# A causal block convolution with one shared product per head, block halves in a new order, and re-paced shared-expert steps

## The chip, the cores and the metric

The kernel runs on one core of one Trainium2 chip. The metric is the device time of one execution in microseconds (us). Engines are named as in the profile: PE is TensorE (PEld its weight loads), DVE is VectorE, ACT is ScalarE, POOL is GpSimd, SP is the engine that issues most DMAs.

## What is computed

The input x is (8, 256, 512): batch, channels, sequence. All arithmetic is float32. A layer norm gives v. The channels form 32 heads (groups) of 8. In each group every pair (i, j) of channels is multiplied along the sequence, convolved causally with the group's filter k (by FFT in the reference), a skip term is added, and the result is weighed with the context and summed over i:

```python
kv = vr[:, :, :, None, :] * x2r[:, :, None, :, :]
y = causal_conv(kv, k[group]) + kv * skip
out = jnp.einsum('bhijl,bhil->bhjl', y, x1r)      # x1 = x2 = ctx
x = x + out
```

Then comes a mixture of experts on the layer norm of x, for 2048 tokens of width 512: a shared expert of inner width 704, and eight experts of inner width 352, two of them picked for each token with weights from sigmoid scores:

```python
shared = silu(xf @ wg.T) * (xf @ wu.T) @ wd.T
routed = sum over the two picked experts e of weight_e * (silu(xf @ wg_e.T) * (xf @ wu_e.T)) @ wd_e.T
x = x + shared + routed
```

## The kernel before

**Stages.** The conv stage is a Python loop over heads h = 0 to 31 (L835 to L904), with tile t = h // 2 holding two heads. A tail (L907 to L992) finishes the shared expert and the routing, and then 36 to 39 blocks of routed tokens pass through the experts (L1091 to L1123). This text is about the conv stage. The order on each engine is the order in which the program issues instructions[...].

**The convolution as products.** The 512 positions are 4 blocks of 128. Convolution with a filter is multiplication with a lower triangular Toeplitz matrix: out_lb is the sum over mb <= lb of T(lb - mb) times x_mb, where x_mb is kv of block mb (128 positions by 512 columns of batch, j, i). Six of the ten block products lie below the diagonal and are full (128 x 128 matrices, L406). The four on the diagonal are triangular: each is done as a product of all 128 rows with 64 columns and one of 64 rows with 64 columns (diagonal(), L388 to L394), so that pieces for different column halves and row halves of the array can be in it together. Half blocks are stored turned (reversed) or straight, so that one table of half-lag matrices per head, tz (L52 to L56), serves all products: SIN and SOUT say which blocks of the input and output are turned, BIN in which order the input blocks are stored.

**One head.** make_kv (L349) builds kv on GpSimd two heads ahead, four products of 128x512. conv_products (L364) issues 14 products on TensorE into two PSUM tiles of two banks each, pss[0] and pss[1]; their order is at L400. weigh (L409) on VectorE multiplies such a tile with the context (L416, 1024 elements a partition) and sums over i (L425); pss[0] is weighed when its blocks 0 and 1 are done, pss[1] at the end. Between the two weighs VectorE does other work of the head: in odd heads the residual and its statistics (L859 to L867), in even heads the skip's addition and two transposes (L869 to L873), and in some the routing (L874 to L878). At the end of an odd head VectorE sums the skip (skip_sum, L447) and ScalarE turns the halves of that sum (skip_turn, L456, copies at L462).

**The PSUM tiles** of the tag "acc" are three buffers of two banks (L109), given out in order to the conv's two tiles, to each up step and to each pair of down steps. A new owner waits until the earlier owner's readers are done.

**Shared-expert steps.** The tokens come in 4 chunks of 4 tiles. Each chunk has 6 up steps (up_step, L616: 8 products of 128x512 into one PSUM pair; the sixth has half of them), and 4 down steps (down_step, L663: 5 products each, and after each second one two more). An up step's sigmoid is issued on ScalarE at L640; the multiplications that read its PSUM (L643 to L654) are put on the list "owed", and are issued on VectorE by settle() (L705) ahead of the next head's products or of the next step. Chunk c may start in head 8c + 10. The list of steps is L700 to L703, 40 in all, and the loop at L892 issues them so that (h - 9) * 5 // 4 are done after head h: one in most heads, two in every fourth.

**Routing.** For each chunk c, with r = (h - 10) % 8: r = 0 logits, r = 1 a transpose, r = 2 scores and picks (route_scores, route_pick), r = 3 ranks, r = 4 places, with eight scatter DMAs on GpSimd.

The helper that orders the halves on the host, _orders, is at L1126.

Of the kernel before, what the change touches and what calls it, by code (L numbers as in the profile page):

```python
# [8 lines left out]
F32 = mybir.dt.float32  # L9
I32 = mybir.dt.int32  # L10
AF = mybir.ActivationFunctionType
ALU = mybir.AluOpType
# [3 lines left out]
P = 128  # L16
B, D, L = 8, 256, 512
NH = 8
# [26 lines left out]


HP = P // 2
SIN, SOUT = (0, 1, 0, 1), (0, 1, 1, 0)
BIN = (2, 3, 0, 1)


STRAIGHT, TURNED = (6, 7, 2, 3, 2, 5, 4), (4, 5, 3, 2)  # L52
TZ = [(d, d - 1) for d in STRAIGHT] + [(d - 1, d) for d in TURNED] + [(1, 0), (0, 1)]
NTZ = len(TZ) * HP
TZ_AT = {(0, 3): 0, (2, 3): 2, (0, 1): 3, (0, 2): 5, (1, 3): 7, (1, 2): 9}
TZ_10, TZ_01 = 11, 12  # L56
EPS = 1e-5
CTXBUFS, TZBUFS = 5, 3
WARM = 6
# [4 lines left out]
def tile_xattn_moe(  # L64
# [275 lines left out]
        transposed(xfT_of(t), xn2.pop(t).rearrange("p k q a -> p (k q a)"), f"f_{t}")  # L340


    kvs = {}

    def head_cols(h):
        t, hh = divmod(h, 2)
# [2 lines left out]
    def make_kv(h):  # L349
        if h >= H:  # L350
            return
        t, cols = head_cols(h)
        kv = cvp.tile([P, NLB, B, NH, NH], F32, tag="kv", name=f"kv_{h}")
        for mb in range(NLB):
            at = BIN.index(mb)
            G.tensor_tensor(  # L356
                kv[:, mb],
                vT[t][:, at, :, cols].unsqueeze(2).to_broadcast([P, B, NH, NH]),
                ctxT[t][:, at, :, cols].unsqueeze(3).to_broadcast([P, B, NH, NH]),
                ALU.mult,  # L360
            )
        kvs[h] = kv

    def conv_products(h):  # L364
        kv, tz = kvs.pop(h).rearrange("p k b j i -> p k (b j i)"), tzs.pop(h)
        pss = [
            ps_acc.tile([P, 2, B, NH, NH], F32, tag="acc", name=f"cv_{h}_{n}") for n in range(2)
        ]
        banks = [pss[lb // 2][:, lb % 2].rearrange("p b j i -> p (b j i)") for lb in range(NLB)]
        half = slice(0, HP), slice(HP, P)  # L370
        whole = slice(0, P)

        left = [[lb + 1] * 2 for lb in range(NLB)]

        def product(lb, mb, at, rows, cols):
            here = [n for n in range(2) if cols.start <= n * HP < cols.stop]
            first = left[lb][here[0]] == lb + 1
            for n in here:
                left[lb][n] -= 1
            T.matmul(  # L380
                banks[lb][cols],
                lhsT=tz[rows, at * HP : (at + len(here)) * HP],
                rhs=kv[rows, mb],
                start=first,
                stop=left[lb][here[0]] == 0,
            )

        def diagonal():  # L388

            for lb in range(NLB):  # L390
                product(lb, lb, TZ_01 if SIN[lb] else TZ_10, whole, half[1 - SOUT[lb]])

            for lb in range(NLB):
                product(lb, lb, TZ_10 if SIN[lb] else TZ_01, half[SIN[lb]], half[SOUT[lb]])  # L394

        if h == 0:

            order = [(0, 1), (0, 2), (0, 3), (1, 2), (1, 3), None, (2, 3)]
        else:
            order = [None, (0, 1), (0, 2), (1, 2), (0, 3), (1, 3), (2, 3)]  # L400
        for pair in order:
            if pair is None:
                diagonal()
            else:
                mb, lb = pair
                product(lb, mb, TZ_AT[pair], whole, whole)  # L406
        return pss

    def weigh(h, n, ps):  # L409

        t, cols = head_cols(h)
        if h % 2 == 0 and n == 0:
            convT[t] = cvp.tile([P, NLB, B, R], F32, tag="conv", name=f"convT_{t}")
        prod = cvp.tile([P, 2 * B, NH, NH], F32, tag="prod", name=f"prod_{h}_{n}", bufs=1)
        two = slice(2 * n, 2 * n + 2)
        V.tensor_tensor(  # L416
            prod,
            ps.rearrange("p k b j i -> p (k b) j i"),
            ctxT[t][:, 2 + 2 * n : 4 + 2 * n, :, cols]
            .rearrange("p k b i -> p (k b) i")  # L420
            .unsqueeze(2)
            .to_broadcast([P, 2 * B, NH, NH]),
            ALU.mult,
        )
        V.tensor_reduce(  # L425
            convT[t][:, two, :, cols].rearrange("p k b j -> p (k b) j"), prod, AX.X, ALU.add
        )
# [157 lines left out]
    def route_places(c):  # L585
        def rt(name, s=shape, dtype=F32):
            return small.tile(s, dtype, tag=name, name=f"{name}_{c}")

        sel, entry, _ = picks.pop(c)
        ps = ranks.pop(c)  # L590
        pos = ps[:, :TPC]
        V.tensor_tensor(pos, pos, place.unsqueeze(1).to_broadcast(shape), ALU.add)
        V.tensor_tensor(place, place, ps[:, TPC], ALU.add)
        for n in range(2):
            at, to = rt("at"), rt(f"to{n}", [P, TPC], I32)
            V.tensor_tensor(at, pos, sel[n], ALU.mult)  # L596
            with nc.allow_low_precision(reason="whole numbers below 2**14"):
                V.tensor_reduce(to, at, AX.X, ALU.add)
            for i in range(TPC):
                ins = G.indirect_dma_start(  # L600
                    out=table,
                    out_offset=bass.IndirectOffsetOnAxis(ap=to[:, i : i + 1], axis=0),
                    in_=entry[:, i, n, :],
                    in_offset=None,
                    bounds_check=P * NCOL - 1,
                    oob_is_err=True,
                )
                tc.declare_no_dep(ins.ins, group="table", reason="no two rows have one place")
                tc.add_to_no_dep_group("table", ins.ins)
                scatters.append(ins)  # L610
# [52 lines left out]
    def down_step(c, i):  # L663
# [33 lines left out]

        owed.append(rest)

    steps = []  # L700
    for c in range(NCHUNK):
        steps += [(8 * c + 10, up_step, c, ft) for ft in range(NSF)]
        steps += [(8 * c + 10, down_step, c, i) for i in range(TPC)]  # L703

    def settle():  # L705
        while owed:
# [128 lines left out]
    for h in range(H):  # L835
        t, odd = divmod(h, 2)

        load_toeplitz(h + 2)
        if not odd:
            load_tile(t + 3)  # L840
            load_residual(t - 1)
        elif t == NT - 1:
            load_residual(t)
        if h == 3:
            load_shared()

        if not odd:
            first_sums(t + 2)
        elif t + 2 < NT:
            first_norm(t + 2)  # L850
            quarters(("v", t + 2), xv_d[t + 2])
        c, r = divmod(h - 10, 8)
        if c >= 0 and r == 2:
            route_scores(c)
        settle()
        pss = conv_products(h)
        weigh(h, 0, pss[0])
        if odd and t > 0:
            add_residual(t - 1)  # L859
            mv = small.tile([P, V.BN_AGGR_DIM], F32, tag="mv", name=f"mv_{h}")  # L860
            stats(mv, f"2_{t}", x2[t - 1])
            rt = root(f"2_{t}", mv[:, 1:2], 1.0)
            V.reciprocal(rt, rt)
            nb = small.tile([P, 1], F32, tag="nb", name=f"nb2_{t}", bufs=3)
            V.tensor_scalar(nb, mv[:, 0:1], rt, -1.0, ALU.mult, ALU.mult)
            second_norm(t - 1, (rt, nb))
            quarters(("f", t - 1), xn_d[(t - 1) * P : t * P, :])  # L867
        if not odd and t > 0:
            add_skip(t - 1)  # L869
            if t + 1 < NT:  # L870
                square_vT(t + 1)
            if t > 1:
                square_xfT(t - 2)  # L873
        if c >= 0:  # L874
            if r == 2:
                route_pick(c)
            if r == 4:
                route_places(c)  # L878
        weigh(h, 1, pss[1])
        if odd or h == 0:  # L880
            skip_sum(t + odd)
            skip_turn(t + odd)
        if h == 0:
            make_vT(1)

        if not odd:
            skip_spread(t)
        make_kv(h + 2)
        if not odd:
            skip_products(t + 1)  # L890

        while done < min((h - 9) * 5 // 4, len(steps)) and steps[done][0] <= h:  # L892
            settle()
            step()

        if not odd and t > 0:
            residual_T(t - 1)
        if c >= 0:
            if r == 0:
                route_logits(c)  # L900
            if r == 1:
                route_T(c)
            if r == 3:
                route_ranks(c)  # L904
# [221 lines left out]
def _orders():  # L1126

    import numpy as np

    l = np.arange(L).reshape(NLB, 2, HP)  # L1130
    ins = [l[mb, ::-1] if SIN[mb] else l[mb] for mb in BIN]
    outs = [l[lb, ::-1] if SOUT[lb] else l[lb] for lb in range(NLB)]
    return [np.concatenate(o).reshape(L) for o in (ins, outs)]


# [76 lines left out]
```

## Time and profile before

| | us |
|---|---|
| median of 3 runs | 814.59 (814.1 to 818.03) |
| profiled execution, device time | 815.22 |
| its span, first to last instruction | 813.5 |
| TensorE busy in the span | 787.3 |
| VectorE busy | 504.3 |
| GpSimd busy | 431.0 |
| ScalarE busy | 167.0 |
| conv products (L380), busy | 267.9, in 896 records |
| up steps (L626) / down steps (L670), busy | 156.4 / 70.6 |
| first conv product to last conv product starts | 9.9 to 444.4 |

A line of the timeline gives start, duration, engine, source line, operation, output tile <- input tiles, shape of the first instruction, and x the number of records that it merges. A float32 product is two records on TensorE. A line of the waits reads: engine, tile and line that waited <- engine, tile and line that ended the wait: total us, how often, longest. In groups of instructions, the number after the bar is busy time, then the mean of one in ns.

### The profile page before, as it was taken

The page shows a single profiled execution, that of the slowest core. Times are in us where ns is not written, and L with a number is a line of the kernel's source. Part 1 is how long each engine was busy: PE and PEld are TensorE (multiplying, and loading weights), DVE is VectorE, ACT ScalarE, POOL GpSimd, SP SyncE. Part 2 cuts the span into 40 slices and gives each one's busy share as a digit, 9 for nine tenths or more (in the row PEclk, how much of TensorE's full clock was granted, in tenths as well). Part 3 has the DMA queues.
Part 4 walks back from the last instruction along what each step waited for, and adds up shares of the span by engine and source line. Part 5 has one row for each costly group of instructions (what it writes and reads, how often), then busy time and mean ns, then how long its engine had stood idle before and what let it go on. Part 6 is the DMA issues. An engine that isn't in the chain of part 4 may idle for free. (4 is left out here: it accounts for less than half of the span.)

```text
span 813.5 us, 8376 instructions
## 1 busy us (share of the span) xinstructions
PE 787.3 (97%) x2423; PEld 364.9 (45%) x2423; DVE 504.3 (62%) x1165; ACT 167.0 (21%) x317; POOL 431.0 (53%) x430
## 2 busy tenths in 40 slices
PE   7999999999999999999999999999999999999991
PEld 4333334443434443434344344455555555555550
DVE  2869856655545736744647243359888788788850
ACT  2222233332204132113111110001111111111110
POOL 7767752319550508723504012766777777777521
PEclk9999999999999999999999999999999999999996
DMA  6486433214433122431110392267444334443332
GB/s 231 153 295 205 159 127 114 80 60 70 148 113 119 52 87 60 152 106 58 49 52 4 142 427 95 71 209 199 75 75 74 66 75 75 75 74 69 65 42 31
DMA packets 52141, 90.14 MB, mean 111 GB/s; under 512 B 8832, under 2 KB 24064, under 8 KB 50944
## 3 DMA queue, kind: packets, MB, share of 16 engines
q1 hardware_dynamic: 36960, 62.82, 23.0%
q0 software_dynamic: 10816, 18.92, 12.7%
q10 hardware_dynamic: 4320, 7.87, 3.2%
q8 instruction: 21, 0.34, 0.2%
q14 instruction: 24, 0.20, 0.1%
HBM read 67.39 MB, written 22.18 MB: 110 GB/s over the span
## 5 line engine op out<-in xcount | busy, mean ns | idle before, releaser
L380 PE MATMUL cv<-kv,tz 128*128 128x512 f32 (+2 forms) x896 | 267.9, 608 | 1.8 <-POOL kv L356 1.8
L955 POOL DMA_INDIRECT xg<-xn_d,src x144 | 147.2, 1022 | 57.9 <-issue 39.4
L1014 PE MATMUL up<-wgu_sb,xT 128*128 (+1 forms) x576 | 176.1, 459 | 0.0
L356 POOL TENSOR_TENSOR kv<-vT,ctxT 128x512 f32<-128x512 f32 x128 | 132.5, 1068 | 72.5 <-issue 67.5
L380 PEld LDWEIGHTS cv<-kv,tz 128*128 128x128 f32 (+2 forms) x896 | 93.1, 158 | 162.9 <-issue 151.7
L626 PE MATMUL gu<-xfT,wsh 128*128 128x512 f32 x352 | 156.4, 599 | 0.3
L1058 DVE STREAM_TRANSPOSE hTb<-h 32x96 f32<-32x96 f32 (+1 forms) x560 | 146.3, 261 | 8.2
L1014 PEld LDWEIGHTS up<-wgu_sb,xT 128*128 128x128 f32 x576 | 109.2, 190 | 70.5 <-issue 16.4
L416 DVE TENSOR_TENSOR prod<-cv,ctxT 128x1024 f32<-128x1024 f32 x64 | 77.9, 1217 | 69.3 <-PE cv L380 69.2
L626 PEld LDWEIGHTS gu<-xfT,wsh 128*128 128x128 f32 x352 | 66.9, 192 | 85.6 <-issue 82.6
L600 POOL DMA_INDIRECT table<-entries,to x32 | 31.9, 998 | 135.4 <-DVE at L596 126.9
L1072 PE MATMUL y<-wd_sb,hTb 128*128 (+3 forms) x216 | 98.6, 593 | 0.8 <-ACT hTb L1047 0.8
L1081 POOL DMA_INDIRECT out_dram<-ys,row x36 | 58.2, 1617 | 44.2 <-ACT ys L1080 20.5
L425 DVE TENSOR_REDUCE convT<-prod 128x128 f32<-128x1024 f32 x64 | 78.1, 1220 | 2.2
L670 PE MATMUL dn<-wshd,hT 128*128 128x512 f32 x160 | 70.6, 593 | 0.0
L1072 PEld LDWEIGHTS y<-wd_sb,hTb 128*128 128x128 f32 (+1 forms) x216 | 41.0, 190 | 43.1 <-issue 34.7
L643 DVE TENSOR_TENSOR sg<-sg,gu 128x512 f32<-128x512 f32 (+1 forms) x24 | 16.4, 684 | 64.9 <-ACT sg L640 64.9
L1022 ACT ACTIVATE h<-up 128x352 f32<-128x352 f32 x36 | 16.7, 464 | 164.2 <-PE up L1014 164.2
L640 ACT ACTIVATE sg<-gu 128x512 f32<-128x512 f32 (+1 forms) x24 | 14.3, 596 | 173.4 <-PE gu L626 173.4
L470 POOL TENSOR_TENSOR skip<-ctxT,w 128x512 f32<-128x512 f32 x16 | 18.2, 1136 | 59.0 <-ACT w L462 58.9
L670 PEld LDWEIGHTS dn<-wshd,hT 128*128 128x128 f32 x160 | 30.2, 190 | 37.6 <-issue 37.6
L1023 DVE TENSOR_TENSOR h<-h,up 128x352 f32<-128x352 f32 x36 | 18.6, 517 | 41.3 <-ACT h L1022 41.3
(136 smaller groups left out, 430.7 us busy)
## 6 DMA issues: line engine op xcount, KB each, us to landing
tz<-in_toep_dram SPq DMA_DIRECT2D x32, 416.0 KB, 3.3
wgu_sb<-in_egu_dram SPq DMA_DIRECT2D x8, 1408.0 KB, 17.6
ctxT<-in_cT_dram SPq DMA_DIRECT2D x16, 384.0 KB, 5.0
x<-in_xv_dram SPq DMA_DIRECT2D x16, 256.0 KB, 3.6
x<-in_x_dram SPq DMA_DIRECT2D x16, 256.0 KB, 4.9
xn_d<-xn ACTq DMA_DIRECT2D x16, 256.0 KB, 2.0
out_dram<-x SPq DMA_DIRECT2D x16, 256.0 KB, 2.3
wd_sb<-in_ed_dram SPq DMA_DIRECT2D x8, 512.0 KB, 11.0
```

The costliest lines, as they stand in the source:

```text
L356: G.tensor_tensor(kv[:, mb], vT[t][:, at, :, cols].unsqueeze(2).to_broadcast([P, B, NH, NH]), ctxT[t][:, at, :, cols].unsqueeze(3).to_broa ...
L380: T.matmul(banks[lb][cols], lhsT=tz[rows, at * HP : (at + len(here)) * HP], rhs=kv[rows, mb], start=first, stop=left[lb][here[0]] == 0,)
L416: V.tensor_tensor(prod, ps.rearrange("p k b j i -> p (k b) j i"), ctxT[t][:, 2 + 2 * n : 4 + 2 * n, :, cols] .rearrange("p k b i -> p (k b ...
L425: V.tensor_reduce(convT[t][:, two, :, cols].rearrange("p k b j -> p (k b) j"), prod, AX.X, ALU.add)
L600: ins = G.indirect_dma_start(out=table, out_offset=bass.IndirectOffsetOnAxis(ap=to[:, i : i + 1], axis=0), in_=entry[:, i, n, :], in_offse ...
L626: T.matmul(ps, lhsT=wsh[:, k, m0 : m0 + m], rhs=rhs[k], start=(k == 0), stop=(k == NLB - 1))
L670: T.matmul(ps, lhsT=hTs[c][:, ft, i * P : (i + 1) * P], rhs=wshd[:, ft, :], start=(ft == 0), stop=False,)
L955: G.indirect_dma_start(out=xgs[k][:, c, :], out_offset=None, in_=xn_q, in_offset=bass.IndirectOffsetOnAxis(ap=src[:, c, k : k + 1], axis=0 ...
L1014: T.matmul(ps[:, m, :FF], lhsT=xTs[k][:, j].rearrange("p c b -> p (c b)"), rhs=wk[:, bass.ds(eks[k] * NGU + (m * NLB + j) * FF, FF)], star ...
L1058: V.transpose(hT[q * Q : (q + 1) * Q, :n, c], hk[c * Q : (c + 1) * Q, q * NF * Q : (q * NF + n) * Q].rearrange("p (t a) -> p t a", a=Q),)
L1072: T.matmul(ps, lhsT=hT[:fw, ft].rearrange("p c b -> p (c b)"), rhs=wk[:fw, bass.ds(eks[k] * NWD + ft * L, L)], start=(ft == 0), stop=(ft = ...
L1081: G.indirect_dma_start(out=out, out_offset=bass.IndirectOffsetOnAxis(ap=row[:, k : k + 1], axis=0), in_=y, in_offset=None, bounds_check=NT ...
```

## The change

From head 10 (H9) on, two of the six full products, T2 x0 (for block 2) and T2 x1 (for block 3), become one product, T2 (x0 + x1), in a PSUM tile "same" of its own. What that adds wrongly is put right in the T1 and T3 products: block 2 gets (T1 - T2) x1 in place of T1 x1, block 3 gets (T3 - T2) x0 in place of T3 x0. So five full products are issued rather than six.

- GpSimd makes x0 + x1 (ks) and the two differences (td, with two buffers) at the end of make_kv.
- ScalarE copies "same" to SBUF, once straight for block 2 and once with its halves swapped for block 3, since block 3's output is stored the other way round.
- VectorE adds these copies to the banks of blocks 2 and 3 at the start of weigh.
- The half blocks are laid out anew (SIN, BIN, a new BOUT, the table TZ with 12 entries rather than 13), so that x0 and x1 are stored straight. One PSUM tile now holds blocks 0 and 2, the other blocks 1 and 3.
- In heads 1 to 9 the order is diagonal, (0,2), (1,2), (0,1), (0,3), (1,3), (2,3). From head 10 it is: the shared product, (0,1), (2,3), (T3 - T2) x0, diagonal, (T1 - T2) x1.
- From head 10 VectorE does both weighs after the head's other work, pss[1] first; in heads with route_pick the transpose of xf comes after them.
- The first two chunks' down steps are issued two at a time, which makes 36 steps, and the loop issues one step a head, two in the last.

```diff
-SIN, SOUT = (0, 1, 0, 1), (0, 1, 1, 0)
-BIN = (2, 3, 0, 1)
-STRAIGHT, TURNED = (6, 7, 2, 3, 2, 5, 4), (4, 5, 3, 2)
+SIN, SOUT = (0, 0, 1, 1), (0, 1, 1, 0)
+BIN, BOUT = (1, 3, 0, 2), (0, 2, 1, 3)
+STRAIGHT, TURNED = (6, 7, 4, 5, 3, 2, 5, 4), (2, 3)
...
-TZ_AT = {(0, 3): 0, (2, 3): 2, (0, 1): 3, (0, 2): 5, (1, 3): 7, (1, 2): 9}
-TZ_10, TZ_01 = 11, 12
+TZ_AT = {(0, 3): 0, (1, 3): 2, (0, 1): 4, (1, 2): 4, (0, 2): 6, (2, 3): 8}
+TZ_10, TZ_01 = 10, 11
+H9 = 10
...
         kvs[h] = kv
+        if h >= H9:
+            ks = rows.tile([P, L], F32, tag="xg", name=f"ks_{h}")
+            flat = kv.rearrange("p k b j i -> p k (b j i)")
+            G.tensor_tensor(ks, flat[:, 0], flat[:, 1], ALU.add)
+            td = cvp.tile([P, 2, P], F32, tag="td", name=f"td_{h}", bufs=2)
+            tb = tzs[h][:, : 4 * P].rearrange("p (n m q) -> p n m q", n=2, m=2)
+            G.tensor_tensor(td, tb[:, :, 0], tb[:, :, 1], ALU.subtract)
+            kss[h] = ks, td
...
+        nine = h >= H9
+        if nine:
+            ks, td = kss.pop(h)
+            same = ps_acc.tile([P, 2, L], F32, tag="acc", name=f"same_{h}")[:, 0]
+        pss = {
+            n: ps_acc.tile([P, 2, B, NH, NH], F32, tag="acc", name=f"cv_{h}_{n}")
+            for n in ((1, 0) if nine else (0, 1))
+        }
...
-            order = [None, (0, 1), (0, 2), (1, 2), (0, 3), (1, 3), (2, 3)]
+            order = [(0, 1), (2, 3)]
+            T.matmul(same, lhsT=of(TZ_AT[0, 2]), rhs=ks, start=True, stop=True)
+            again, turned = [
+                rows.tile([P, L], F32, tag="xg", name=f"{name}_{h}") for name in ("same", "turned")
+            ]
+            for n in range(2):
+                A.copy(turned[half[n]], same[half[1 - n]])
+            A.copy(again, same)
+            boths[h] = {2: again, 3: turned}
...
+        if nine:
+            product(3, td[:, 0], kv[:, 0])
+            diagonal()
+            product(2, td[:, 1], kv[:, 1])
         return pss
...
+        for i, lb in enumerate(BOUT[2 * n : 2 * n + 2]):
+            if lb in boths.get(h, ()):
+                bank = ps[:, i].rearrange("p b j i -> p (b j i)")
+                V.tensor_tensor(bank, bank, boths[h].pop(lb), ALU.add)
...
+    def down_steps(c, i, n):
+        for j in range(i, i + n):
+            down_step(c, j)
+
     steps = []
     for c in range(NCHUNK):
         steps += [(8 * c + 10, up_step, c, ft) for ft in range(NSF)]
-        steps += [(8 * c + 10, down_step, c, i) for i in range(TPC)]
+        n = 2 if c < NCHUNK - 2 else 1
+        steps += [(8 * c + 10, down_steps, c, i, n) for i in range(0, TPC, n)]
...
-        weigh(h, 0, pss[0])
+        nine, picks_here = h >= H9, c >= 0 and r == 2
+        if not nine:
+            weigh(h, 0, pss[0])
...
+        if nine:
+            weigh(h, 1, pss[1])
+            weigh(h, 0, pss[0])
+            if picks_here:
+                square_xfT(t - 2)
+        else:
+            weigh(h, 1, pss[1])
...
-        while done < min((h - 9) * 5 // 4, len(steps)) and steps[done][0] <= h:
+        while done < h - 9 + h // (H - 1) and steps[done][0] <= h:
```

More of the change, by code (lines that the diff above doesn't have):

```diff
@@ L340, in make_xfT @@
         transposed(xfT_of(t), xn2.pop(t).rearrange("p k q a -> p (k q a)"), f"f_{t}")
-    kvs = {}
+    kvs, kss, boths = {}, {}, {}
     def head_cols(h):
@@ L362, in make_kv, with product @@
         kvs[h] = kv
+        if h >= H9:
[6 more added lines that the diff above has]
+            kss[h] = ks, td
     def conv_products(h):
         kv, tz = kvs.pop(h).rearrange("p k b j i -> p k (b j i)"), tzs.pop(h)
[L366 to L369, printed above, removed]
+        nine = h >= H9
[6 more added lines that the diff above has]
+        }
+        places = [BOUT.index(lb) for lb in range(NLB)]
+        banks = [pss[n // 2][:, n % 2].rearrange("p b j i -> p (b j i)") for n in places]
         half = slice(0, HP), slice(HP, P)
         whole = slice(0, P)
-        left = [[lb + 1] * 2 for lb in range(NLB)]
-        def product(lb, mb, at, rows, cols):
+        total = [1, 2, 2, 3] if nine else [1, 2, 3, 4]
+        left = [[n] * 2 for n in total]
+        def product(lb, w, x, cols=whole):
             here = [n for n in range(2) if cols.start <= n * HP < cols.stop]
-            first = left[lb][here[0]] == lb + 1
+            first = left[lb][here[0]] == total[lb]
             for n in here:
@@ L381, in product @@
                 banks[lb][cols],
-                lhsT=tz[rows, at * HP : (at + len(here)) * HP],
-                rhs=kv[rows, mb],
+                lhsT=w,
+                rhs=x,
                 start=first,
@@ L386, in product, with of @@
             )
+        def of(at, n=2, rows=whole):
+            return tz[rows, at * HP : (at + n) * HP]
         def diagonal():
             for lb in range(NLB):
-                product(lb, lb, TZ_01 if SIN[lb] else TZ_10, whole, half[1 - SOUT[lb]])
+                product(lb, of(TZ_01 if SIN[lb] else TZ_10, 1), kv[:, lb], half[1 - SOUT[lb]])
             for lb in range(NLB):
-                product(lb, lb, TZ_10 if SIN[lb] else TZ_01, half[SIN[lb]], half[SOUT[lb]])
+                rows = half[SIN[lb]]
+                at = TZ_10 if SIN[lb] else TZ_01
+                product(lb, of(at, 1, rows), kv[rows, lb], half[SOUT[lb]])
         if h == 0:
             order = [(0, 1), (0, 2), (0, 3), (1, 2), (1, 3), None, (2, 3)]
-        else:
-            order = [None, (0, 1), (0, 2), (1, 2), (0, 3), (1, 3), (2, 3)]
+        elif not nine:
+            order = [None, (0, 2), (1, 2), (0, 1), (0, 3), (1, 3), (2, 3)]
+        else:
+            order = [(0, 1), (2, 3)]
[7 more added lines that the diff above has]
+            boths[h] = {2: again, 3: turned}
         for pair in order:
@@ L405, in conv_products @@
                 mb, lb = pair
-                product(lb, mb, TZ_AT[pair], whole, whole)
+                product(lb, of(TZ_AT[pair]), kv[:, mb])
+        if nine:
+            product(3, td[:, 0], kv[:, 0])
+            diagonal()
+            product(2, td[:, 1], kv[:, 1])
         return pss
@@ L411, in weigh @@
         t, cols = head_cols(h)
-        if h % 2 == 0 and n == 0:
+        if t not in convT:
             convT[t] = cvp.tile([P, NLB, B, R], F32, tag="conv", name=f"convT_{t}")
+        for i, lb in enumerate(BOUT[2 * n : 2 * n + 2]):
+            if lb in boths.get(h, ()):
+                bank = ps[:, i].rearrange("p b j i -> p (b j i)")
+                V.tensor_tensor(bank, bank, boths[h].pop(lb), ALU.add)
         prod = cvp.tile([P, 2 * B, NH, NH], F32, tag="prod", name=f"prod_{h}_{n}", bufs=1)
@@ L871, in tile_xattn_moe @@
                 square_vT(t + 1)
-            if t > 1:
+            if t > 1 and not picks_here:
                 square_xfT(t - 2)
[L874 to L879, printed above, removed]
+        if picks_here:
+            route_pick(c)
+        if c >= 0 and r == 4:
+            route_places(c)
+        if nine:
+            weigh(h, 1, pss[1])
+            weigh(h, 0, pss[0])
+            if picks_here:
+                square_xfT(t - 2)
+        else:
+            weigh(h, 1, pss[1])
         if odd or h == 0:
@@ L1131, in _orders @@
     ins = [l[mb, ::-1] if SIN[mb] else l[mb] for mb in BIN]
-    outs = [l[lb, ::-1] if SOUT[lb] else l[lb] for lb in range(NLB)]
+    outs = [l[lb, ::-1] if SOUT[lb] else l[lb] for lb in BOUT]
     return [np.concatenate(o).reshape(L) for o in (ins, outs)]
```

## The prediction, made before the changed kernel ran

> **What bounds the kernel now.** I read the busy shares first, then what TensorE waited for, then its work in order of time around one head.
>
> ```profile
> PE 787.3 (97%) x2423; PEld 364.9 (45%) x2423; DVE 504.3 (62%) x1165; ACT 167.0 (21%) x317; POOL 431.0 (53%) x430
> ```
>
> A busy share alone could mislead, so the next question is whether TensorE ever waits. These are all its waits in the span:
>
> ```profile
> PE slots_ps L788 <- DVE by_quarter L776: 2.0, 1, 2.0
> PE cv L380 <- POOL kv L356: 1.8, 1, 1.8
> PE ptf L272 <- ACT xn_kqa L328: 1.6, 1, 1.6
> PE warm L819 <- POOL filler L143: 1.3, 1, 1.3
> PE ptr L486 <- DVE convT L478: 1.1, 1, 1.1
> PE ptv L272 <- ACT xn L267: 1.0, 1, 1.0
> PE y L1072 <- ACT hTb L1047: 0.8, 1, 0.8
> ```
>
> They come to 9.6 us in 813.5, and none lies in heads 10 to 31 (106 to 445 us). There the end is set by how many products TensorE is given. The timeline of TensorE (start, duration, x records) prices them; this is head 20 and the step after it:
>
> ```profile
> 258.34 8.30 PE L380 MATMUL cv<-kv,tz 128*64 128x512 f32 x28
> 266.48 7.03 PE L626 MATMUL gu<-xfT,wsh 128*128 128x512 f32 x16
> 273.35 0.60 PE L486 MATMUL ptr<-ident,convT 128*128 128x128 f32 x4
> 273.88 8.30 PE L380 MATMUL cv<-kv,tz 128*64 128x512 f32 x28
> ```
>
> Use starts, since ends overlap. An up step is 8 products in 16 records, so a float32 product is two records: (273.35 - 266.48)/8 = **0.859 us** a product. A head's conv is 8.14 us; less six products (5.15) the diagonal costs 2.99, where its four 128x64 and four 64x64 products would need 2.58 if two, or four, ran at once. So they do run together, with 0.4 us of switching.
>
> The last view is the end of an odd head on ScalarE (head 19), which the pace of the steps will touch:
>
> ```profile
> 254.65 0.45 ACT L462 COPY w<-w 64x32 f32<-64x32 f32 x2 [2.16 <-DVE w L452]
> 255.11 1.28 ACT L640 ACT_TABLE_LOAD   x1
> 258.01 0.60 ACT L640 ACTIVATE sg<-gu 128x512 f32<-128x512 f32 x1 [1.61 <-PE gu L626]
> ```
>
> The sigmoid of an odd head's step stands behind skip_turn's copies, which stand behind VectorE's skip_sum, which stands behind the last weigh; then the table load. Here TensorE is still later (1.61 us idle), so nothing is lost.
>
> [...]the eight diagonal products take 2.99 us, not 8 x 0.859. [...] The trace has the 1.28 and no further gap: a square root follows its load at once (170.60 + 1.28, next at 171.89). [...] L490, 128x512 from PSUM, takes 676 ns, and I use that for the new adds.
>
> **The change part by part.**
>
> *Products.* Heads 10 to 31 issue 13 products instead of 14, with the diagonal's eight unchanged in number and shape: 22 x 0.859 = **-18.9 us**, all on TensorE's path. Heads 0 to 9 keep 14. The new order of halves changes the order of the four 64x64 tiles from (0,0),(1,1),(0,1),(1,0) to (0,0),(0,1),(1,1),(1,0): still four different tiles and four banks. I take zero; bounds: zero, and the rival below. A gain is excluded but for the 0.4 us of switching, whose number of switches is the same.
>
> *Added on GpSimd.* x0 + x1 (128x512) like L356, 1.07 us; T1 - T2 and T3 - T2 (128x256) between half of that and all of it, say 0.6: 1.7 us a head. GpSimd needs about 12.2 us in two heads of some 30, and has kv two heads ahead; both hide. The new wait, td for its slot until head h's last product, has only skip_products and the next kv behind it, due a head later.
>
> *Added on ScalarE.* Three copies from PSUM like L507 (0.59, started every 0.5): 1.6 us a head. They free "same", whose buffer the step's product takes at 7.28 us after the conv's start (8.14 - 0.86). In even heads the queue ahead is sigmoid and sums, over at about 4.1; free at 5.8. In a head with route_scores (12, 20, 28) another load and sigmoid precede, and the odd head's late sigmoid (below) shifts the sums: free near 7.6, so TensorE waits 0.3 x 3 = **+0.9**.
>
> *Added on VectorE.* Two adds of 0.68 a head. A weigh is now 0.70 + 1.25 + 1.14 = 3.1 us. Take the conv's start as 0: the diagonal ends at 3.43 + 2.99 = 6.42, weigh 1 runs 6.6 to 9.7, weigh 0 to 12.8 (its bank read out by 11.7). The next head asks for that bank at 0.86 into its conv. With a full step that is 7.28 + 6.87 + 0.86 = 15.0: covered by 3.3 us of the step; without a step it would cost 3.6 a head. With route_pick ahead (4.0 us, from 5.9 on) it is read out by 15.0, asked for at 15.5: still covered.
>
> *The pace.* One step a head puts the short sixth up step (four products, 3.43 us) in heads 15, 23 and 31, **odd** heads. Before it fell to even heads (177.37, 305.02). Now follow the chain in head 15: weigh 0 ends 12.8, skip_sum 0.68 to 13.5, skip_turn 0.45 to 13.95, table load to 15.25, sigmoid to 15.85, VectorE's three products of L643 and L649 (0.69 + 0.86) to **17.5**. Only then is the step's PSUM free. TensorE has ended conv and step at 10.7, and head 16's fifth product group, the diagonal, asks for that buffer at 10.7 + 3.43 = **14.1**. It waits 3.4 us with the whole queue behind it. Heads 15 and 23: **+6.7**; head 31 has no skip_sum and no head after it, so nothing. Other odd heads with up steps (11, 13, 19, 21, 27, 29) have the same chain, ending near 17.3, and the next diagonal due at 18.1 or later: 0.8 us of cover. Bounds of one stall: 0 (if head 16 were served by another buffer) and 5 us (if copies and adds run slower).
>
> *Moved.* The down pairs are the same products in heads 16, 17, 24, 25 rather than spread; their outputs' DMAs on SP's queue stand behind the same Toeplitz load. The table shrinks from 13 to 12 columns of halves (416 to 384 KB a head): DMA is not waited for, 0. In heads 1 to 9 weigh 0 starts one product later (0.86): the one wait there, 1.1 us at L486, ends a VectorE backlog that began at a DMA wait, so 0. After head 31 the same 13 steps are left (40 - 27 before, 36 - 23 after), all shifted; the experts' weights land before a product waits for them (no wait at L1014).
>
> **Sum:** -18.9 + 6.7 + 0.9 = -11.3. The profiled execution took 815.2 (span 813.5 and 1.7 around it): 803.9. The median of the runs is 0.6 lower: **803.3**.
>
> **Rivals.**
>
> *A, as summed*, 803.3, with its own range 800 to 806.5.
>
> *B, the short step's chain is covered*: something in it starts earlier than I queue it. Then only the products count: 814.6 - 18.9 = 795.7. For it: TensorE loses nothing now. Against: the order on ScalarE shown above.
>
> *C, the VectorE and ScalarE chain is about 1 us longer than I count* (adds and copies meeting GpSimd's added work; L478, without PSUM, varies from 0.68 to 1.59 us). Then six more odd heads lose 0.2 each, heads 15 and 23 one more each, the three routing heads one more each: + 6.2, 809.5. Against: VectorE's busy share is 62%.
>
> *D, slower: the four 64x64 tiles lose their overlap.* In the new order neighbours share rows or columns; before, first and second, third and fourth shared neither. If they went two by two, each of 32 heads pays one product more, 32 x 0.86 = 27.5: 831. It decides from 0.35 us a head on, where it eats the 11.3. Against: the 128x64 products share all rows and overlap.
>
> That the change does not do what it says is excluded: 13 products are issued where 14 were.
>
> **How the numbers follow.** A 0.57, B 0.17, C 0.20, D 0.06. Half a percent, about what a measurement can tell here, is 4.1 us: 810.5 to 818.7 is "same". A and B are faster, C in six parts of ten: 0.86. The rest of C, 0.08, is same; D 0.06 is slower. The range takes A whole, most of B and C: 796 to 809.8.
>
> **What would show it.** TensorE's timeline: heads from 10 on at 26 records and 7.3 us; 2.99 for the diagonal unchanged in all heads (else D). TensorE's waits: a wait of 3 to 4 us at the diagonal of heads 16 and 24 for VectorE's L649 (none: B; also at heads 12, 14, 20: C), and small ones at the steps of heads 12, 20, 28 for the copies. VectorE's new adds at 0.68. GpSimd never ahead of a TensorE wait. I am wrong if a wait for td or the sum appears, or if the tail after head 31 is not merely shifted.

## The result and the profile after

| | before | changed |
|---|---|---|
| median, us (4 runs each) | 816.31 (814.1 to 818.29) | 807.03 (806.57 to 809.01) |
| ratio to before, 95% interval | | 0.9892 (0.9855 to 0.9929) |
| profiled execution: device time / span | 815.22 / 813.5 | 809.01 / 807.2 |
| from the first transpose of a residual (tile 0) to the last tile's transpose "ptf", in the trace | 423.6 | 417.3 |

The change makes the kernel 1.1% faster: 9.3 us, where 11.3 were forecast. The last row, the **conv stage** below, covers heads 3 to 31. It leaves out the first heads and the tail, where the granted clock of TensorE (the share of full speed that it is given) differed between the two profiled executions: its mean was 0.84 from 9 to 20 us before and 0.73 from 9 to 21.5 us after, 0.83 in the tail before (503 to 513 us) and 1.00 after (500 to 507 us).

The shares of busy time in the changed kernel:

```profile
PE 774.5 (96%) x2379; PEld 355.0 (44%) x2379; DVE 532.8 (66%) x1209; ACT 212.8 (26%) x389; POOL 473.2 (59%) x474
```

TensorE gave up 44 records, two for each of 22 products. Its busy time fell by 12.8 us, its span by 6.3: the rest is in new waits. These are the first two of all its waits (engine, tile and line that waited <- who ended the wait: total us, times, longest):

```profile
PE cv L398 <- DVE hT L693: 6.2, 2, 3.1
PE gu L670 <- ACT same L435: 2.1, 3, 1.5
```

The first is the wait that the sum had priced at 6.7 us. Of the second, 1.5 us lie in head 10, which the sum had not looked at. TensorE's timeline shows head 11, which follows the logits; head 13 with the transposes ahead of it; then the short step of head 15 and the conv of head 16:

```profile
116.06 1.06 PE L543 MATMUL pl<-xfT,gw_sb 128*32 128x512 f32 x8
117.06 1.12 PE L429 MATMUL same<-ks,tz 128*128 128x512 f32 x2
...
124.54 7.03 PE L670 MATMUL gu<-xfT,wsh 128*128 128x512 f32 x16
...
146.67 0.60 PE L530 MATMUL ptr<-ident,convT 128*128 128x128 f32 x4
147.10 1.02 PE L429 MATMUL same<-ks,tz 128*128 128x512 f32 x2
147.97 1.88 PE L398 MATMUL cv<-kv,tz 128*128 128x512 f32 x4
149.68 1.02 PE L398 MATMUL cv<-kv,td 128*128 128x512 f32 x2
150.63 2.96 PE L398 MATMUL cv<-kv,tz 128*64 128x512 f32 x16
153.52 1.13 PE L398 MATMUL cv<-kv,td 128*128 128x512 f32 x2
154.48 7.03 PE L670 MATMUL gu<-xfT,wsh 128*128 128x512 f32 x16
...
184.52 3.60 PE L670 MATMUL gu<-xfT,wsh 128*128 128x512 f32 x8
187.96 1.02 PE L429 MATMUL same<-ks,tz 128*128 128x512 f32 x2
188.83 1.98 PE L398 MATMUL cv<-kv,tz 128*128 128x512 f32 x4
190.65 1.02 PE L398 MATMUL cv<-kv,td 128*128 128x512 f32 x2
194.76 5.60 PE L398 MATMUL cv<-kv,tz 128*64 128x512 f32 x16 [3.09 <-DVE hT L693]
200.29 1.23 PE L398 MATMUL cv<-kv,td 128*128 128x512 f32 x2
```

Head 13 takes 154.48 - 147.10 = 7.38 us, against 8.14 before: 0.76 less, not 0.86. The transposes ahead of it take 147.10 - 146.67 = 0.43, against 273.88 - 273.35 = 0.53 before: there is the other 0.1. Head 11 takes 124.54 - 117.06 = 7.48. Head 16 stops at its diagonal for 3.1 us, as predicted, and then the sixteen records of the diagonal last 5.53 us in place of 2.89. That second loss was not in the prediction. The view by stretches shows what it is (its columns: busy time of PE, PEld, DVE, ACT and POOL with the number of instructions, then TensorE's granted clock, DMA share, GB/s):

```profile
21.50:190.00 168.50, 166.09 (x556) 63.71 (x555) 126.15 (x184) 61.46 (x124) 115.12 (x109) 1.00 0.45 146
...
194.70:201.00 6.30, 6.24 (x18) 1.63 (x19) 2.36 (x4) 3.33 (x5) 4.96 (x5) 0.54 0.18 66
```

After the wait the granted clock is about half: 0.54 in this stretch, 1.00 in the first. The cause of the wait is read on ScalarE, the end of head 15, and on VectorE:

```profile
190.66 0.45 ACT L506 COPY w<-w 64x32 f32<-64x32 f32 x2 [7.05 <-DVE w L496]
191.12 1.28 ACT L684 ACT_TABLE_LOAD   x1
192.41 0.59 ACT L684 ACTIVATE sg<-gu 64x512 f32<-64x512 f32 x1
```

```profile
189.95 0.68 DVE L496 TENSOR_REDUCE w<-skip 128x64 f32<-128x512 f32 x1
193.04 0.68 DVE L687 TENSOR_TENSOR sg<-sg,gu 64x512 f32<-64x512 f32 x1 [2.42 <-ACT sg L684]
193.75 0.86 DVE L693 TENSOR_TENSOR hT<-sg,gu 64x256 f32<-64x256 f32 x2
```

The step's products were over at about 188.1 (TensorE began the next head at 187.96). Their sigmoid starts at 192.41, behind the copies and the table load, and VectorE frees the PSUM at 194.6; TensorE goes on at 194.76.

**Theories.** Theory 1: the gain is the 22 products; what is missing of it is the odd head's queue behind a short step, because four tiles a head now go round three PSUM buffers and the conv therefore takes the step's buffer. Rival 2: VectorE, with both weighs at the head's end, is simply late, whatever ScalarE does. Others stand with the runs.

### The profile page after: what moved, and what is told of

It reads as the page before. It is cut to its first block, busy times and chain, and to the rows that moved or that the text cites. A ratio compares the mean times of both kernels' runs of the same rounds, so it can differ in the third digit from the quotient of the medians.

```text
span 807.2 us, 8497 instructions
## 1 busy us (share of the span) xinstructions
PE 774.5 (96%) x2379; PEld 355.0 (44%) x2379; DVE 532.8 (66%) x1209; ACT 212.8 (26%) x389; POOL 473.2 (59%) x474
## 3 DMA queue, kind: packets, MB, share of 16 engines
q0 software_dynamic: 10816, 18.92, 12.9%
## 5 line engine op out<-in xcount | busy, mean ns | idle before, releaser
L398 PE MATMUL cv<-kv,tz 128*64 128x512 f32 (+2 forms) x720 | 197.8, 629 | 8.0 <-DVE hT L693 6.2
L1073 PEld LDWEIGHTS up<-wgu_sb,xT 128*128 128x128 f32 x576 | 109.2, 190 | 70.5 <-issue 16.6
L398 PEld LDWEIGHTS cv<-kv,tz 128*64 128x64 f32 (+2 forms) x720 | 62.5, 154 | 131.6 <-issue 111.1
L460 DVE TENSOR_TENSOR prod<-cv,ctxT 128x1024 f32<-128x1024 f32 x64 | 78.1, 1221 | 21.8 <-PE cv L398 20.2
L469 DVE TENSOR_REDUCE convT<-prod 128x128 f32<-128x1024 f32 x64 | 78.1, 1220 | 2.2
L398 PE MATMUL cv<-kv,td 128*128 128x512 f32 x88 | 47.4, 620 | 0.0
L1139 ACT ACTIVATE ys<-y,gate 128x512 f32<-128x512 f32 x36 | 24.8, 688 | 78.3 <-PE y L1131 75.3
```

The lines of the kernel that those rows point to most:

```text
L398: T.matmul(banks[lb][cols], lhsT=w, rhs=x, start=first, stop=left[lb][here[0]] == 0,)
L460: V.tensor_tensor(prod, ps.rearrange("p k b j i -> p (k b) j i"), ctxT[t][:, 2 + 2 * n : 4 + 2 * n, :, cols] .rearrange("p k b i -> p (k b ...
L469: V.tensor_reduce(convT[t][:, two, :, cols].rearrange("p k b j -> p (k b) j"), prod, AX.X, ALU.add)
L1073: T.matmul(ps[:, m, :FF], lhsT=xTs[k][:, j].rearrange("p c b -> p (c b)"), rhs=wk[:, bass.ds(eks[k] * NGU + (m * NLB + j) * FF, FF)], star ...
```

## The experiments

Each kernel was compared with the kernel before on the same chip. There were three chips, on which the kernel before had medians of 814.8, 823.6 and 834.0 us; so across chips only ratios and conv stages compare (e1 to e4 ran on the first, e5 to e8 on the second, e9 to e12 on the third). Each conv stage is read from one trace. "Waits" are TensorE's in the conv stage, us, without those of up to 1 us ahead of the transposes. e1's and e2's edits are called the two mends.

| run | edit | median / before | ratio (95%) | conv stage | waits for L693, L689 | other waits |
|---|---|---|---|---|---|---|
| e1 | short step even, all chunks | 802.72 / 814.78 | 0.9854 (0.9826 to 0.9882) | 407.3 | 0.8 | copies 2.1 |
| e2 | turn after the step | 797.87 / 814.78 | 0.9810 (0.9774 to 0.9845) | 408.5 | 1.2 | copies 1.5 |
| e3 | copies first in even heads | 809.16 / 814.78 | 0.9925 (0.9898 to 0.9953) | 414.4 | 6.4 | 1.2 in head 10 |
| e4 | pace alone, on the kernel before | 816.55 / 814.78 | 1.0011 (0.9996 to 1.0025) | 422.1 | 0 | 0 |
| e5 | both mends | 809.44 / 823.56 | 0.9820 (0.9794 to 0.9846) | 405.8 | 0 | copies 1.5 |
| e6 | first weigh not last | 861.84 / 823.56 | 1.0462 (1.0432 to 1.0493) | 458.5 | 10.2 | 30 |
| e7 | shared product in the other pool | 811.40 / 823.56 | 0.9844 (0.9822 to 0.9867) | 407.3 | 0 | 3.7 |
| e8 | shared product from head 4 | 836.50 / 823.56 | 1.0149 (1.0122 to 1.0175) | 430.4 | 6.2 | 19 |
| e9 | the changed kernel again | 822.27 / 834.03 | 0.9860 (0.9821 to 0.9899) | 414.1 | 6.2 | copies 2.1 |
| e10 | short step even, three chunks | 814.36 / 834.03 | 0.9760 (0.9722 to 0.9799) | 407.6 | 0.8 | copies 2.1 |
| e11 | e2 again | 818.85 / 834.03 | 0.9807 (0.9762 to 0.9851) | 408.3 | 1.2 | copies 1.5 |
| e12 | e5 again | 811.52 / 834.03 | 0.9739 (0.9696 to 0.9782) | 406.2 | 0 | copies 1.5 |

**e1: the short step in an even head.**

```diff
-        steps += [(8 * c + 10, up_step, c, ft) for ft in range(NSF)]
+        steps += [(8 * c + 10, up_step, c, ft) for ft in (0, 1, 2, 3, 5, 4)]
```

> The changed kernel with one edit: each chunk's up steps go in the order 0, 1, 2, 3, 5, 4, so the short step falls on an even head (r = 4) and a full one on the odd head (r = 5). Theory 1 (the stall is the odd head's queue: weighs, skip_sum, skip_turn, table load, sigmoid, then the products that free the step's PSUM): no wait of TensorE for VectorE's L693 (6.2 us before the edit), so no half clock after it (about 4.3 us in the profiled execution): 797 to 801 us. Rival 2 (VectorE is simply late after two weighs at the head's end, whatever ScalarE does): a wait of about 3 us at the diagonal moves to the heads after r = 4, time unchanged near 807.

The waits of 3.1 us went; 0.53 and 0.3 us are left, and after the first of these the diagonal takes 191.73 - 188.85 = 2.88 us, so no half clock follows it. The conv stage is 10 us shorter. Rival 2 falls for the even heads: in head 14 VectorE has two weighs at the end too, and freed the short step's PSUM at 173.72, 0.28 us before the next diagonal started. Odd heads, where skip_sum comes on top, are left to e2. The time, 802.72, is above the 797 to 801 expected. A reason lies in the tail: there the same edit puts the short step beside the load of the routing table, and TensorE waits for that load.

```profile
PE slots_ps L836 <- DMA tab<-table: 3.5, 1, 3.5
```

**e2: the turn after the step.**

```diff
-            skip_turn(t + odd)
+            if not nine:
+                skip_turn(t + odd)
...
+        if nine and odd:          # after the loop that issues the step
+            skip_turn(t + 1)
```

> The changed kernel with skip_turn's two copies issued after the head's step instead of before it, from head 10 on; nothing else. Theory 1: the sigmoid of heads 15 and 23 comes 0.2 us after its products (10.9 us after the conv's start, not 15.3), VectorE's products then only wait for skip_sum (13.5) and end near 15.1, one us after the diagonal asks: each of the two waits falls from 3.1 to about 1 us, and with it the half clock after it: 799 to 803 us. Rival 2: waits stay at 3.1, 807.

On ScalarE, the end of head 15 in this run:

```profile
180.97 1.28 ACT L684 ACT_TABLE_LOAD   x1 [0.39 <-ACT xn L269]
185.14 0.59 ACT L684 ACTIVATE sg<-gu 64x512 f32<-64x512 f32 x1 [2.88 <-PE gu L670]
187.64 0.44 ACT L506 COPY w<-w 64x32 f32<-64x32 f32 x2 [1.91 <-DVE w L496]
```

The table is loaded early and the sigmoid waits for nothing but its products. TensorE's wait at the diagonal of head 16 is now 0.58 us, for VectorE's skip_sum and the two weighs ahead of the products. VectorE has the same work in the same order as in the changed kernel, so of 3.1 us, 2.5 were ScalarE's queue, and Rival 2 is left with the 0.58. The waits for the copies in heads 12 and 20 fell from 0.3 to about 0.1, as expected if the odd head's late sigmoid had pushed them.

**e3: the copies ahead of the statistics.**

```diff
         if not odd:
-            first_sums(t + 2)
+            if h < H9:
+                first_sums(t + 2)
...
         pss = conv_products(h)
+        if not odd and h >= H9:
+            first_sums(t + 2)
```

> The changed kernel with the even heads' statistics of the next tile (first_sums, ScalarE) issued after the conv's products, so the copies of the shared product stand ahead of them. Theory 1: TensorE's three waits for the copies (L435, 2.1 us, longest 1.5 in head 10) go, the two waits for L693 stay at 3.1: 805 us. Rival 3 (these waits are ScalarE's total load): they come back at another line of ScalarE, 807.

Neither a gain of 2 us nor a loss can be told from the changed kernel here (the intervals overlap). In heads 12 and 20 the wait is gone. In head 10, where it was 1.48, 1.17 is left: the copies now end at 105.0 and the step starts at 106.87, for its input xf is transposed on VectorE until 106.77. One wait had covered another. In the changed kernel this transpose ends at 108.22, 0.3 us ahead of the step, after a wait for a DMA:

```profile
107.51 0.71 DVE L296 STREAM_TRANSPOSE xfT<-xq_f 128x512 f32<-128x512 f32 x1 [2.13 <-DMA xq_f<-xn_d]
```

(For head 10 of this run the profile names ScalarE's L253, which ended at about the same time. At the two diagonals, 3.2 us stand against the copy L435. VectorE's L693 ended 0.2 us before that copy, at 192.31, so that one or the other releases.)

**e4: the pace alone, in the kernel before.** The edit is the change's down_steps, its list of steps and its "h - 9 + h // (H - 1)", without the shared product.

> The kernel before, with only the new pace: down steps by twos in the first two chunks and one step a head, two in the last. Theory 1: the late products of the odd head matter only because four tiles a head now go round three PSUM buffers, so that the conv's tile takes the step's buffer; here three tiles a head go round three buffers and a step only waits for the step before: no wait of TensorE at the conv, time as before, 816 within 2. Rival 4 (the pace itself costs): waits of about 3 us at heads 16 and 24, 820 or more.

No wait and no difference. The pace costs nothing that can be told by itself; it needs the fourth tile to cost something.

**e7: the shared product in another pool.** This takes the fourth tile out of the three buffers and leaves the pace.

```diff
-            same = ps_acc.tile([P, 2, L], F32, tag="acc", name=f"same_{h}")[:, 0]
+            same = ps_tp.tile([P, L], F32, tag="tp", name=f"same_{h}")
```

> The changed kernel with the shared product's PSUM tile taken from the two one-bank buffers of the transposes instead of the three pairs of banks, so that again three tiles a head go round three buffers there. Theory 1: no wait for L693 and none for the copies at the steps (8.3 us of waits go, and the half clock after them); new waits of about 2.3 us at the shared product in heads 11, 19 and 27, whose buffer the residual of the head before still holds: 801 to 804. Rival 2 (VectorE late by itself): waits at the diagonal of heads 16 and 24 stay, 810 or more.

The waits for L693 are gone, and new ones stand at the shared product of heads 11, 19 and 27, at 0.75 each instead of 2.3. I had named the residual as the reader that holds the buffer. The times name another: the shared product starts at 116.00, 237.71 and 359.41, each 0.1 us after ScalarE's copy of the logits (L551) ends, while the residual of head 11 is read until 116.49. In head 10 a wait of 1.4 us stays although no copy holds the step's buffer: as in e3, xf is late there (its transpose ends at 106.61, the step starts at 106.71). With e4 this settles that the buffer's rotation joins the conv to the step.

```profile
PE same L429 <- issue: 2.3, 3, 0.8
PE gu L670 <- issue: 1.4, 1, 1.4
```

**e6: the first weigh where it was.** The weigh of blocks 1 and 3 is issued right after the products; the rest of the head's work, square_xfT included, follows, then the other weigh.

> The changed kernel with one part undone: from head 10 on the first weigh (blocks 1 and 3) stands where it stood before, ahead of the head's other VectorE work, and only the second stands last. VectorE then sits idle until the diagonal ends (6.6 us into the conv) and does the other work after it. Theory 1, by queue: the first up step of a chunk waits for its input, transposed at about 11.8 and asked for at 7.3 (heads 10, 18, 26: 4.5 each), heads with picks 2 each, odd heads 1.2 to 1.8, heads 15 and 23 5.8: in all some 40 us of waits against 8.3, about 835 to 850. Rival 5 (VectorE has so much time that its order does not matter): 807 to 812.

TensorE's waits in the conv stage come to 40 us, as queued, though 6.8 of them are at a place I had not named, the shared product waiting for GpSimd's sum. A lower clock came on top: its mean from 100 to 470 us was 0.96, and the step after the wait of 5.97 us took 122.14 - 112.41 = 9.73 us against 6.87. The kernel is 4.6% slower than the one before. This order of VectorE's work carries the change.

```profile
PE gu L670 <- DVE xfT L296: 8.5, 2, 4.3
PE same L429 <- POOL ks L368: 6.8, 2, 3.5
PE gu L670 <- issue: 6.0, 1, 6.0
PE cv L398 <- DVE hT L689: 5.9, 5, 1.5
PE cv L398 <- DVE hT L693: 4.3, 2, 2.8
```

**e8: from head 4 on**, H9 = 4 and nothing else.

> The changed kernel with the shared product from head 4 on instead of head 10. Heads 4 to 9 have no step beside them. If only products counted: six heads by 0.7, 803. Theory 1 (the step is the cover of VectorE's work): VectorE needs 15.4 us for two such heads now and 18.2 with the four new adds, TensorE 15.5: VectorE sets the pace, 18.2 against 16.9 without the shared product, so 3 times 1.3 more: 810 to 813, with waits of TensorE for VectorE's weighs in heads 5 to 9.

Expected was a time 2 to 5 us below the kernel before (810 to 813 against 814.8); it is 12.9 us above. Heads 8 and 9 (78.1 to 99.1 us) take 21.1 us, not 18.2. VectorE is busy for only 16.6 of 21: its queue stands still behind ScalarE, 2.0 us for the turned copy in each even head and 2.0 for the root in each odd one, since both stand behind other work there.

```profile
DVE rstd L917 <- ACT rstd L244: 6.5, 4, 2.1
DVE cv L457 <- ACT turned L434: 6.1, 3, 2.0
```

That VectorE's work is uncovered without a step holds (10.2 us of TensorE's waits are for its L460); the size was off by ScalarE's part.

**e5: both mends**, with e1's order in the first three chunks only.

> The changed kernel with both mends: skip_turn's copies after the step (as in the run with the late turn), and the short step in the even head in the first three chunks only, so that the last chunk keeps a full step beside the load of the table. Theory 1: no wait for VectorE over 0.5 us at heads 15 to 16 and 23 to 24, the wait for the table stays at 2 us, one wait of 1.5 us in head 10: 796 to 798 us, about 1 us below the late turn alone. Rival 2 (VectorE late by itself): waits of 1 us or more stay at the diagonal, 798 or more.

No wait for VectorE is left in the conv stage, which is 17.8 us shorter than before. The time is 14.1 us below the kernel before, where 17 to 19 were expected (796 to 798 against the first chip's 814.8): in the trace TensorE waits 4.9 and 3.6 us at the start of the experts' blocks.

**e9 to e12** put the changed kernel and the mends on one chip.

> The changed kernel itself, once more, as the measure for the three runs beside it on one chip: 1.0 to 1.4 per cent below the kernel before, two waits of 3.1 us for L693 and 2.1 us for L435.

> The changed kernel with the short up step in an even head in the first three chunks, the last chunk in its old order; skip_turn stays before the step. Theory 1: as with the short step even in all chunks, waits for L693 gone (0.5 us at most left, for L689), but the wait for the table, 3.5 us there, falls back to about 2 and no half clock follows: 1 to 4 us below that run, 8 to 9 us below the changed kernel. Rival (the table's load was late by chance there): the same time as with all four chunks, 12 us below the kernel before.

> The changed kernel with skip_turn's copies after the step, again, beside the other two mends on one chip: 8 to 9 us below the changed kernel, waits of 0.6 us at heads 16 and 24 and none above 0.2 at heads 12 and 20.

> The changed kernel with both mends, beside each alone on one chip. Theory 1: the late turn has already taken 2 x 2.5 of the 2 x 3.1 us and the short waits of heads 12 and 20, so the second mend adds about 1.2 us: 9 to 10 us below the changed kernel. If the two waits were separate causes, their gains would add: 16 us below.

e9 repeats the changed kernel's gain (1.4%) and its waits. By medians on that chip e10, e11 and e12 lie 7.9, 3.4 and 10.8 us below the changed kernel, where 8 to 9, 8 to 9, and 9 to 10 were expected; by conv stage 6.5, 5.8 and 7.9. In the conv stage the mends do not add (6.5 + 5.8 = 12.3 against 7.9): they are two ways past one queue. The medians alone do not show it (7.9 + 3.4 = 11.3 against 10.8). In e12 head 16 runs through:

```profile
186.34 1.02 PE L429 MATMUL same<-ks,tz 128*128 128x512 f32 x2
187.20 1.88 PE L398 MATMUL cv<-kv,tz 128*128 128x512 f32 x4
188.91 1.02 PE L398 MATMUL cv<-kv,td 128*128 128x512 f32 x2
189.87 2.96 PE L398 MATMUL cv<-kv,tz 128*64 128x512 f32 x16
```

e11 gained less in time than in the conv stage: in its trace TensorE waits 11.6 us at the start of the experts' blocks. Waits there come to 6 to 12 us in every trace of the second and third chip, e12's too, and to 1.4 at most on the first. Their cause stays open: in e5 and e12 an add of L739 on VectorE starts 10 and 19 us late, with no releaser that the program shows. In e10 the wait for the table fell from 3.5 us (e1) to 0.5, but the tail was shorter by 0.9 us only; why was not shown.

e12 has the lowest ratio to the kernel before, 2.6% faster, though its interval overlaps e10's; against the changed kernel on that chip it is 1.3% faster by medians.

## Why the prediction was right

The direction, the mechanism and the place of the largest loss were right; the gain was forecast 2.0 us too large. (The time itself, 807.03, lies 3.7 us above the forecast, 1.7 of them because the median of the kernel before rose from 814.59 to 816.31 with its fourth run. It also lies just above the range of Rival A, 800 to 806.5.) In the two profiled executions the sum was further off: -6.3 against -11.3. Term by term, with each wait counted from the start that was due, 0.1 to 0.2 us longer than its idle time:

- **Products**, -18.9 forecast, -17.4 measured. The step that failed is "whose number of switches is the same". It holds where transposes stand ahead of the head: the switch of tile form into the diagonal moved from them into the head, where the full product before the diagonal lasts 150.63 - 149.68 = 0.95 in place of 0.86 (the one after it, 154.48 - 153.52 = 0.96, took as long in the kernel before), and 0.76 + 0.1 is the 0.86 of the forecast. It fails where a product of another form stands ahead, the logits or the down steps' last products: it was followed by the diagonal and is now followed by a full product, which is one switch more. Five such heads take 7.48 us, 0.2 above the forecast 7.28; the three after the ranks lose 0.1 each.
- **Pace**, +6.7 forecast (its own terms add up to 17.4 rather than 17.5 us, that is 6.5): +6.3 in two waits, at the heads and for the reason given. The half clock after them (granted 0.54 from 194.7 to 201.0 us, 0.76 from 320 to 327), +2.7 and +1.6 us (the stretch from the diagonal to the next step, 6.59 and 5.45 against 3.85), was **left out**. It is the largest error of the sum.
- **Copies**, +0.9 forecast for heads 12, 20 and 28: 0.5, 0.5 and none (no statistics are due in head 28), but 1.6 in head 10, which I had not looked at. There xf is late as well, as e3 and e7 show, so the copies' own part is about 0.3. Together +2.6.
- **Order of the tiles** (D), 0: the diagonal lasts 2.89 us in the changed kernel. D is out. B is out with the waits; C's further waits did not come.
- **GpSimd**, hidden: no wait behind td or ks, though the sum took 1.29 us and not 1.07, and the differences 0.73 and not 0.6.
- **Not counted**: waits of 0.8 us in the kernel before (for xf at heads 10, 18 and 26) and 1.4 us at L486 and L328 shrank or went; and the clock outside the conv stage, which cost 1.8 us more in the first head (0.73 against 0.84) and 1.7 us less in the tail (1.00 against 0.83). I take this last pair for chance, which was not shown.

-17.4 + 6.3 + 4.3 + 2.6 - 0.8 - 1.4 = -6.4, against 417.3 - 423.6 = -6.3 for the conv stage; the first head and the tail cancel, and the spans differ by -6.3 too. The medians give -9.3: the changed kernel's profiled execution was the slowest of its four (809.01, with a granted clock of 0.982 against 0.984 to 0.986 in the others), and that of the kernel before was 1.1 us below its median. So it is in part luck that the forecast came as near as 2.0 us.

## What to carry to other kernels

When a product is taken out of a TensorE-bound loop, count the PSUM tiles that go round in a turn before and after: one tile more can tie the next product to a reader three engines away, although no engine is full. Follow that reader's queue on every engine for each kind of head, including the first. Here a short step on the wrong parity cost 10 us of the conv stage, more than the 6.3 that were left of its gain, and moving two small copies behind a sigmoid gave 8.8 of them back. A wait of TensorE should be priced with the half clock that may follow it: here two waits of 3.1 us cost 2.7 and 1.6 us more.

## What the runs showed of the hardware

- What followed a wait of TensorE at a diagonal differed. In the changed kernel, after 3.09 us in heads 16 and 24, the granted clock was 0.54 from 194.7 to 201.0 us and 0.76 from 320 to 327, and the two cost 2.7 and 1.6 us more. In e3, after 3.19 us in head 16, the diagonal took 198.09 - 192.56 = 5.53 us, as long as in the changed kernel. In e6, after 2.77 us in that head, it took 214.49 - 211.60 = 2.89 us, as long as without a wait.
- After the wait of 1.48 us in head 10 of the changed kernel the clock stayed at 1.00 (21.5 to 190 us).
- In the tail, at the routing's product, the wait was 2.03 us in the kernel before (L788); the clock was 0.83 from 503 to 513 us, and the next step's eight records took 512.74 - 507.53 = 5.21 us. In the changed kernel (L838) it was 1.98 us; the clock was 1.00 from 500 to 507 us, and those records took 506.57 - 503.05 = 3.52 us. What decides between the two was not shown.
- Four 64x64 products in the new order start within 20 ns of each other (head 13: all between 152.50 and 152.53 us), as before (head 20: between 260.20 and 260.23). I estimate the three changes of tile form in a head at 0.5 us together: 7.38 us less eight times 0.859, five full products and three for the diagonal, if its products overlap fully.
- A kernel's time differed by up to 19 us between chips (the kernel before: 814.8 to 834.0). In the changed kernel's two traces the conv stage differs by 3 us (417.3 and 414.1) and the experts' blocks by 15 (281.0 and 295.8 from their first product on).
